# The last graph of a two-layer graph-attention kernel: its outputs written half by half in another order, reciprocals spread by ScalarE, and the range check in three parts

## The chip, the core and the metric

The kernel runs on one core of a Trainium2 chip. The core has five engines that run their own instruction streams side by side: TensorE (PE, matrix products; PEld is its loading of weights), VectorE (DVE), ScalarE (ACT), GpSimd (POOL) and SyncE (SP, which here only issues DMAs). They wait for one another through semaphores. SBUF is the on-chip memory with 128 partitions, PSUM the accumulators that TensorE writes. The metric is the device time of one execution in microseconds (us), of which the median of several runs is taken; a smaller number is better.

## What is computed

The input is 64 graphs of 256 nodes with 512 features each, and a 0/1 adjacency matrix for each graph; all is float32. Two attention layers follow one another.

```python
# layer 0
feat_proj = feats @ fc_w.T + fc_b
logits = (feat_proj @ q_w.T + q_b) + transpose(feat_proj @ k_w.T + k_b)
masked = leaky_relu(logits + (1 - adj) * -1e9, 0.01)
x = softmax(masked) @ feat_proj + feats
# layer 1, 8 heads of 64 features
Q, K, V = x @ W_q + b_q, x @ W_k + b_k, x @ W_v + b_v
scores = Q K^T / 8 + (x @ w_g[:D])_i + (x @ w_g[D:])_j + b_g + log(adj + 1e-9)
out = softmax(scores) @ V + x
```

## The kernel before, in words

Two graphs make a group, so there are 32 groups (`NG = 32`, `GP = 2`), and each group has four tiles of 128 nodes (`T = 4`). The loop over groups is unrolled. In step g the group g (called F) goes through layer 0 and the projections of layer 1, while group g-1 (A) goes through most of its attention, group g-2 (D) through what is left of it, and group g+1 (X) has its data loaded. The order of all instructions is written out by hand: strings such as `"pv.p2 scores:0 pv.p6"` name methods of a group, and every engine takes its instructions in exactly this order (`manual_schedule`). The projections are made from seven block products instead of eight (`pv.p1` to `pv.p7`, `Product.add`, line 412), with sums on DVE (`pv.sum_10` and so on, line 443) and copies from PSUM on ACT (line 429).

In the last step (g = 31) there is no group behind, so group 31 finishes its whole attention there. For each graph `gr` (0 or 1) and each half of the heads `hg` (0 or 1):

- `scores:u`, u = 2*gr + hg: PE makes the scores (line 859), ACT the exponentials (line 873);
- `factor:u:jc` multiplies them by the adjacency (DVE, line 879); `both:u` adds the two tiles (DVE, line 886);
- `sums_1:0` and `sums_of_e:1` add the weights over the columns by matmuls (lines 962 and 978), and ACT copies the sums to SBUF (`sms`, lines 969 and 985);
- `attend:gr` makes the weighted sums of values for both halves (PE, line 899), each copied from PSUM to the tile `oTs` by ACT (line 906);
- `ratios_t` transposes the sums in blocks of 32 (DVE, line 1023); `ratios_r` takes their reciprocal (line 996) and spreads it over `recip1` by one copy of all partitions and four of 32 partitions each, which overwrite parts of the first (lines 999 and 1002, all on DVE);
- `finish:gr` does for each half in turn: transposes the attended values (line 1033), multiplies by the reciprocals (line 1034) and adds the residual (line 1040), all on DVE with 512 columns each, and then stores the graph by four DMAs (line 1049), for graph 0 from SyncE's queue, for graph 1 from SyncE's and ScalarE's in turn.

Group 30 (A) finishes its second graph at the start of that stretch: `totals_1 ratios:1` (lines 927 and 942), `turn:1 divide:1 complete:1 store:1` (lines 991, 1011, 1019).

The softmaxes of the fast path take no maximum off. Instead, `in_range` compares every reciprocal with 1e-20 and 1e25 (`is_ge` at line 1058, `is_le` at line 1059), takes the minimum of the outcomes over the columns (line 1063) and the minimum with earlier outcomes (line 1065). `recip0` holds layer 0's reciprocals (4 columns for a group), `recip1` layer 1's (64 columns for a group, four groups at a time). The last call covers groups 30 and 31: 8 columns of layer 0 and 128 of layer 1. Then PE transposes the outcome (line 1096), DVE reduces it and writes an integer flag (lines 1100 and 1101), every engine loads the flag (line 1366) and branches on it (line 1368): a general version of the whole computation runs if any reciprocal was out of range, else the program ends.

The functions that the diff touches follow.

Of the kernel before, what the change touches and what calls it, by code (L numbers as in the profile page):

```python
# [10 lines left out]
F32 = mybir.dt.float32  # L11
I32 = mybir.dt.int32
AF = mybir.ActivationFunctionType
ALU = mybir.AluOpType
# [3 lines left out]
P = 128  # L18
# [7 lines left out]
def kernel(  # L26
# [64 lines left out]
    nc = tc.nc  # L91
    NB, N, D = x.shape
    NH = 8
    HD = D // NH
    B = 32
    RS = P // 4
    NC = D // P
    TPG = N // P
    GP = 2
    T = GP * TPG  # L100
    TOK = GP * N
    NG = NB // GP
# [10 lines left out]
    both = [i for i, a in enumerate(act_sets.SETS) if a.name == "natural_log_exp_and_others"]  # L113
    nc.scalar.add_instruction(
        mybir.InstLoadActFuncSet(
            name=nc.get_next_instruction_name(), act_func_set_id=both[0], ins=[], outs=[]
# [43 lines left out]
    NR = 4  # L160
    recip0 = const.tile([P, NG, T], F32, tag="recip0", name="recip0")
    recip1 = const.tile([P, NR, GP, NC, N // B], F32, tag="recip1", name="recip1")

    def fast():
        main = ExitStack()
        with main:
            one = main.enter_context(tc.tile_pool(name="one", bufs=1))
            wts = main.enter_context(tc.tile_pool(name="wts", bufs=1))
            two = main.enter_context(tc.tile_pool(name="two", bufs=2))
# [9 lines left out]
            def bank(name):  # L179
                return ps.tile([P, 512], F32, tag="bank", name=name)  # L180
# [64 lines left out]
            def columns(rows, cols, name):  # L245

                n = rows.shape[0]
                pt = bank(name)
                nc.tensor.transpose(pt[:, 0:n], rows, ident[0:n, 0:n])
                nc.vector.tensor_copy(cols, pt[:, 0:n])  # L250
# [138 lines left out]
            class Product:  # L389
# [5 lines left out]
                scores = False  # L395
# [133 lines left out]
            class Group:  # L529
# [357 lines left out]

                def attend(self, gr):

                    g = self.g  # L890
                    self.oTs[gr] = one.tile([P, 2, 512], F32, tag="oTs", name=f"oTs_{g}_{gr}")
                    for hg in range(2):
                        po = bank(f"oT_{g}_{gr}_{hg}")
                        oT = po.rearrange("p (r i) -> p r i", r=2)
                        for pr in range(2):
                            for jc in range(TPG):
                                for par in range(2):
                                    h = 4 * hg + 2 * pr + par
                                    nc.tensor.matmul(  # L899
                                        oT[par * HD : (par + 1) * HD, pr, :],  # L900
                                        lhsT=self.v[:, gr * TPG + jc, ts(h, HD)],
                                        rhs=self.e[2 * gr + hg, jc][:, par, pr, :],
                                        start=(jc == 0),
                                        stop=(jc == TPG - 1),
                                    )
                        nc.scalar.copy(self.oTs[gr][:, hg, :], po)  # L906

                def parts(self, u):

# [83 lines left out]
                def ratios_r(self, gr):  # L993
                    g, nb = self.g, N // B
                    rc = two.tile([P, 2, nb], F32, tag="rc", name=f"rc_{g}_{gr}")
                    nc.vector.reciprocal(rc, self.st.rearrange("p (b c) -> p c b", c=B)[:, 0:2, :])

                    rs = recip1[:, g % NR, gr].rearrange("p (h n) b -> p h n b", h=2)
                    nc.vector.tensor_copy(rs, rc.unsqueeze(2).to_broadcast([P, 2, 2, nb]))
                    for q in range(4):  # L1000
                        m = q ^ 1
                        nc.vector.tensor_copy(
                            rs[q * B : (q + 1) * B, :, m % 2, :], rc[m * B : (m + 1) * B]
                        )
                    self.rs = recip1[:, g % NR, gr]
# [16 lines left out]
                    self.st = one.tile([P, N], F32, tag="sms1", name=f"st_{self.g}_{gr}")  # L1022
                    nc.vector.transpose(self.st, self.sms1[gr])

                def finish(self, gr):


                    g, nb = self.g, N // B
                    self.osb[gr] = two.tile([P, NC * N], F32, tag="osb", name=f"osb_{g}_{gr}")
                    for hg in range(2):  # L1030
                        o = self.osb[gr][:, ts(hg, 512)]
                        blocks = o.rearrange("p (m c) -> p m c", c=B)
                        nc.vector.transpose(o, self.oTs[gr][:, hg, :])  # L1033
                        nc.vector.tensor_tensor(  # L1034
                            blocks, blocks,
                            self.rs[:, ts(hg, 2)].rearrange("p n b -> p (n b)").unsqueeze(2).to_broadcast(
                                [P, 2 * nb, B]
                            ), ALU.mult,
                        )
                        nc.vector.tensor_tensor(o, o, self.xb[gr][:, ts(hg, 512)], ALU.add)  # L1040
                    self.store(gr, 2 * (nc.sync, nc.scalar) if gr else 4 * (nc.sync,))

                def store(self, gr, queues=4 * (nc.sync,)):
                    dst = of[ts(self.g * GP + gr, N), :].rearrange(
# [3 lines left out]
                    for q in range(P // B):  # L1048
                        queues[q].dma_start(dst[q], src[q * B : (q + 1) * B])

            def in_range(lo, hi, name):

                n0, n1 = (hi - lo) * T, (hi - lo) * GP * NC * N // B
                ok = one.tile([P, n0 + n1], F32, tag="junk", name=f"ok_{name}")
                for src, a, b in ((recip0[:, lo:hi].rearrange("p g t -> p (g t)"), 0, n0),
                                  (recip1[:, lo % NR : lo % NR + hi - lo].rearrange(
                                      "p g a h b -> p (g a h b)"), n0, n0 + n1)):
                    nc.vector.tensor_scalar(ok[:, a:b], src, R_LOW, None, ALU.is_ge)
                    nc.vector.scalar_tensor_tensor(
                        ok[:, a:b], src, R_HIGH, ok[:, a:b], ALU.is_le, ALU.mult  # L1060
                    )
                okp = const.tile([P, 1], F32, tag=f"okp_{name}", name=f"okp_{name}")
                nc.vector.tensor_reduce(okp, ok, AX.X, ALU.min)
                if "all" in checked:
                    nc.vector.tensor_tensor(okp, okp, checked["all"], ALU.min)
                checked["all"] = okp

            def attention_and_layer_0(D, A, F, X):

# [21 lines left out]

            def check_ranges():

                in_range(NG - NR // 2, NG, "last")
                pk = bank("pok")
                nc.tensor.transpose(pk[0:1, 0:P], checked["all"], ident)

                def flag_ready():
                    oks = one.tile([1, 2], F32, tag="oks", name="oks")
                    nc.vector.tensor_reduce(oks[:, 0:1], pk[0:1, 0:P], AX.X, ALU.min)  # L1100
                    nc.vector.tensor_copy(flag, oks[:, 0:1])

                return flag_ready

            checked = {}

            def step(d, a, f, n, check):


# [13 lines left out]
                D, A, F, X = of(d), of(a), of(f), of(n)  # L1123
# [25 lines left out]
                X("dot_k:2 dot_k:3")  # L1149
                F("turn_residual:0")  # L1150
                if n is None:
                    A("attend:1 totals_1 ratios:1 turn:1 divide:1 complete:1 store:1")
                    F("residual:1 turn_residual:1")

                    F("pv.p2 scores:0 pv.p6 pv.sum_00 factor:0:0 factor:0:1 scores:1 both:0 pv.p7")
                    F("factor:1:0 factor:1:1 both:1 scores:2 pv.p5 sums_1:0 scores:3 pv.sum_11")
                    F("ratios_t:0 ratios_r:0 factor:2:0 factor:2:1 pv.p3 pv.p4 factor:3:0 pv.sum_10")
                    F("factor:3:1 attend:0 finish:0 sums_of_e:1 attend:1")
                    F("ratios_t:1 ratios_r:1 finish:1")
                    check_ranges()()  # L1160
                    return
                X("mask add_eps")
# [7 lines left out]
            with tc.manual_schedule(engines=ENGINES):  # L1170
                f = Group(0)
                f.x, f.a = x_0, adj_0

                warm = bank("warm")
                for n in range(6):
                    nc.tensor.matmul(warm[:, 0:P], lhsT=ident, rhs=ident, start=True, stop=True)
                columns(rows_0, cols_0, "cols_0")
                rows_qk = rows_of_x()
                k_constant = constant()
                d, a, a_w = None, None, {}  # L1180
                for g in range(NG):
                    n = Group(g + 1) if g + 1 < NG else None

                    def check():

                        if d is not None and (d.g % NR == NR - 1 or d.g == NG - NR // 2 - 1):
                            in_range(d.g // NR * NR, d.g + 1, f"{d.g}")

                    step(d, a, f, n, check)
                    d, a, f = a, f, n  # L1190
# [215 lines left out]
```

## Time and profile before

| | us |
|---|---|
| median of 3 runs | 2311.21 |
| lowest and highest of them | 2310.70, 2311.36 |
| the profiled execution's own time | 2310.62 |
| its span, first to last instruction | 2308.80 |
| PE busy in the span | 2294.2 (99%) |
| DVE busy | 2124.2 (92%) |
| ACT busy | 1071.8 (46%) |

The span was taken from one profiled execution by the hardware profiler, so single durations come from that execution. "Busy" is the time in which an engine ran an instruction; loads of registers, branches and semaphore waits aren't counted. The chain of waits follows the work that ended last back from the end: at each step to whatever released an instruction, or to the instruction before it on its engine. In a timeline line, the columns are the start in us, the time in us, the engine, the line of the code, the operation, its output and input tiles with their shapes, and how often it ran in a row; in brackets stands how long the engine was idle before it and what ended that. The engine names with a q (PEldq, DVEq) are the engines' instruction sequencers. The last TensorE product ahead of the final check ends at about 2297.1, the integer flag is written at 2302.82 to 2302.96, and the span ends at 2308.80.

### The profile page before, as it was taken

The page shows a single profiled execution, that of the slowest core. Times are in us where ns is not written, and L with a number is a line of the kernel's source. Part 1 is how long each engine was busy: PE and PEld are TensorE (multiplying, and loading weights), DVE is VectorE, ACT ScalarE, POOL GpSimd, SP SyncE. Part 2 cuts the span into 40 slices and gives each one's busy share as a digit, 9 for nine tenths or more (in the row PEclk, how much of TensorE's full clock was granted, in tenths as well). Part 3 has the DMA queues.
Part 4 walks back from the last instruction along what each step waited for, and adds up shares of the span by engine and source line. Part 5 has one row for each costly group of instructions (what it writes and reads, how often), then busy time and mean ns, then how long its engine had stood idle before and what let it go on. Part 6 is the DMA issues. An engine that isn't in the chain of part 4 may idle for free.

```text
span 2308.8 us, 33613 instructions
## 1 busy us (share of the span) xinstructions
PE 2294.2 (99%) x12618; PEld 1905.2 (83%) x12618; DVE 2124.2 (92%) x3180; ACT 1071.8 (46%) x1865; POOL 121.9 (5%) x120
## 2 busy tenths in 40 slices
PE   9999999999999999999999999999999999999997
PEld 6888888888888888888888888888888888888885
DVE  6899999999999999999999999999999999999997
ACT  3544444454445444454444454444544445444443
POOL 0000000000000000000000000000000000000000
PEclk9999999999999999999999999999999999999999
DMA  4122332223322233232233232332222323223312
GB/s 133 46 61 73 78 76 66 70 61 85 79 73 61 61 78 78 74 68 61 69 78 83 60 75 63 79 78 74 64 60 74 78 73 70 65 64 81 84 46 38
DMA packets 517264, 163.84 MB, mean 71 GB/s; under 512 B 415188, under 2 KB 478696, under 8 KB 517096
## 3 DMA queue, kind: packets, MB, share of 16 engines
q1 hardware_dynamic: 514440, 160.32, 28.8%
q8 instruction: 102, 1.67, 0.3%
q10 hardware_dynamic: 2656, 1.31, 0.2%
q14 instruction: 66, 0.54, 0.1%
HBM read 95.43 MB, written 66.12 MB: 70 GB/s over the span
## 4 chain that ended last, share of the span: by engine, by line
PE 98%; DVE 1%; DMA 0%; ACT 0%; issue 0%; ACTq 0%; DVEq 0%
PE pv L412 17%; PE pq L412 17%; PE pf L412 16%; PE pk L412 16%; PE sc L859 11%; PE oT L899 10%; PE y L689 9%; PE fp L718 1%; DMA fc_nat<-in_L_gnn_fc_w_dram 0%; PE rc L637 0%; DVE osb L1034 0%; PE tot L927 0%; DVE osb L1040 0%; PE xTp L705 0%; DVE osb L1033 0%; DVE x L756 0%
## 5 line engine op out<-in xcount | busy, mean ns | idle before, releaser
L873 ACT ACTIVATE e<-sc,c 128x1024 f32<-128x1024 f32 x254 | 269.0, 1110 | 79.2 <-PE sc L859 77.6
L879 DVE TENSOR_TENSOR e<-e,am 128x1024 f32<-128x1024 f32 x254 | 297.7, 1213 | 0.4 <-ACT e L873 0.4
L859 PE MATMUL sc<-qT,kT 64*128 64x256 f32 x2048 | 255.8, 390 | 0.3 <-ACT e L873 0.3
L899 PE MATMUL oT<-e,v 128*64 128x256 f32 x2032 | 233.4, 382 | 0.0
L859 PEld LDWEIGHTS sc<-qT,kT 64*128 64x128 f32 x2048 | 187.3, 187 | 52.6 <-issue 32.7
L495 POOL TENSOR_TENSOR pf_s<-pf_s,x 128x512 f32<-128x512 f32 x93 | 118.4, 1273 | 2106.1 <-ACT pf_s L494 2038.8
L689 PE MATMUL y<-e,x 128*128 128x256 f32 x992 | 225.6, 381 | 0.0
L899 PEld LDWEIGHTS oT<-e,v 128*64 128x64 f32 x2032 | 140.2, 137 | 85.3 <-issue 10.7
L689 PEld LDWEIGHTS y<-e,x 128*128 128x128 f32 x992 | 186.4, 190 | 23.7
L432 ACT ACTIVATE pq_s<-pq,cols 128x256 f32<-128x256 f32 x192 | 80.5, 470 | 249.1 <-PE pq L412 249.1
L494 ACT ACTIVATE pf_s<-pf,recip 128x256 f32<-128x256 f32 x186 | 77.9, 470 | 197.6 <-PE pf L412 197.6
L917 DVE TENSOR_REDUCE part<-est 128x32 f32<-128x1024 f32 x124 | 151.3, 1220 | 4.3
L916 DVE STREAM_TRANSPOSE est<-es 128x1024 f32<-128x1024 f32 x124 | 152.2, 1227 | 0.0
L886 DVE TENSOR_TENSOR es<-e,e 128x1024 f32<-128x1024 f32 x126 | 149.3, 1205 | 1.1
L695 ACT COPY yT<-y 128x512 f32<-128x512 f32 x124 | 72.6, 585 | 131.7 <-PE y L689 130.9
L429 ACT COPY pk_s<-pk 128x512 f32<-128x512 f32 x96 | 56.3, 586 | 165.7 <-PE pk L412 159.0
L906 ACT COPY oTs<-oT 128x512 f32<-128x512 f32 x128 | 75.0, 586 | 118.0 <-PE oT L899 97.3
L412 PE MATMUL pk<-t1b,wk 128*128 128x256 f32 x512 | 121.1, 380 | 0.4 <-DVE kT L443 0.4
L412 PE MATMUL pv<-wv,t1b_c 128*128 128x256 f32 x512 | 121.1, 380 | 0.0
L412 PE MATMUL pv<-wv,t1b 128*128 128x256 f32 x512 | 121.0, 380 | 0.0
L412 PE MATMUL pq<-x1T,wq 128*128 128x256 f32 x512 | 121.0, 379 | 0.0
L412 PE MATMUL pk<-x1T,wk 128*128 128x256 f32 x512 | 121.0, 379 | 0.0
(181 smaller groups left out, 4506.3 us busy)
## 6 DMA issues: line engine op xcount, KB each, us to landing
x<-in_x_dram SPq DMA_DIRECT2D x32, 1024.0 KB, 5.1
out_dram<-osb SPq DMA_DIRECT2D x254, 128.0 KB, 3.1
xd<-xt SPq DMA_DIRECT2D x124, 256.0 KB, 2.0
x1T<-xd SPq DMA_DIRECT2D x496, 64.0 KB, 1.9
adj<-in_adj_dram SPq DMA_DIRECT2D x128, 128.0 KB, 3.5
qrow<-q SPq DMA_DIRECT2D x31, 256.0 KB, 3.9
fc_nat<-in_L_gnn_fc_w_dram ACTq DMA_DIRECT2D x4, 256.0 KB, 3.8
wq<-in_L_gnn_W_q_dram SPq DMA_DIRECT2D x1, 1024.0 KB
```

The costliest lines, as they stand in the source:

```text
L412: nc.tensor.matmul(o, lhsT=lk[:, ts(m, P)] if len(lk.shape) == 2 else lk[:, m], rhs=rk, start=(start and m == 0 and k == 0), stop=(m == 1 ...
L432: nc.scalar.activation(dst[:, m], src[:, m], AF.Identity, bias=self.bias[:, 2 * o + m : 2 * o + m + 1],)
L494: nc.scalar.mul(s[:, m], src[:, m], self.recip[:, TPG * k + m : TPG * k + m + 1])
L495: nc.gpsimd.tensor_tensor(s, s, self.out(o, k), ALU.add)
L689: nc.tensor.matmul(y[:, ts(gr, N)], lhsT=self.x[:, gr * TPG + j, ts(c, P)], rhs=self.e0[:, j, gr, :], start=(gr == 0 and j == 0), stop=(gr ...
L859: nc.tensor.matmul(sc[:, par, pr, :], lhsT=self.kT[rows, 2 * hg + pr, ts(t, P)], rhs=self.qT[rows, 2 * hg + pr, ts(gr, N)], start=True, st ...
L873: nc.scalar.activation(e, sc, AF.Exp, bias=self.c[:, t : t + 1], scale=SCALE)
L879: nc.vector.tensor_tensor(ef, ef, self.am[:, jc, u // 2, :].unsqueeze(1).to_broadcast([P, 4, N]), ALU.mult,)
L886: nc.vector.tensor_tensor(self.esum[u], self.e[u, 0], self.e[u, 1], ALU.add)
L899: nc.tensor.matmul(oT[par * HD : (par + 1) * HD, pr, :], lhsT=self.v[:, gr * TPG + jc, ts(h, HD)], rhs=self.e[2 * gr + hg, jc][:, par, pr, :],
L916: nc.vector.transpose(turned, self.esum[u].rearrange("p a b i -> p (a b i)"))
L917: nc.vector.tensor_reduce(self.part[:, hg, :], turned.rearrange("p (m c) -> p m c", c=B), AX.X, ALU.add,)
```

## The change

Four things are edited, all of which act in the last step only.

- `attend` and `finish` are cut into units of one half: `attend_unit`, `turn_unit` (transpose into the output tile), `finish_unit` (multiply and add). The new order in the last step is: both halves of graph 0 attended, half 0 turned and finished, half 1 turned; then the sums of graph 1, their transpose and reciprocals; then half 1 of graph 0 finished and graph 0 stored; then for graph 1: half 0 attended and turned, half 1 attended, half 0 finished, half 1 turned and finished, stored.
- In `ratios_r` the five copies that spread the reciprocals are given to ScalarE instead of VectorE, for both graphs. The reciprocal itself stays on VectorE.
- `in_range` takes any list of sources. Its last call is cut in three: "late" (layer 0 of groups 30 and 31 and layer 1 of the first graph of group 30) ahead of group 30's `attend:1`, "later" (the second graph of group 30) behind `both:1`, and "last" (group 31, 64 columns) where the single call was.
- `finish_unit` reads `recip1` by its own index instead of the attribute `self.rs`.

The order of the units on PE stays as it was. The diff, cut to its core:

```diff
                 def attend(self, gr):
+                    for hg in range(2):
+                        self.attend_unit(gr, hg)
+
+                def attend_unit(self, gr, hg):
...
-                    nc.vector.tensor_copy(rs, rc.unsqueeze(2).to_broadcast([P, 2, 2, nb]))
+                    nc.scalar.copy(rs, rc.unsqueeze(2).to_broadcast([P, 2, 2, nb]))
                     for q in range(4):
                         m = q ^ 1
-                        nc.vector.tensor_copy(
+                        nc.scalar.copy(
                             rs[q * B : (q + 1) * B, :, m % 2, :], rc[m * B : (m + 1) * B]
                         )
...
-                def finish(self, gr):
...
+                def turn_unit(self, gr, hg):
+                    if hg == 0:
+                        self.osb[gr] = two.tile(
+                            [P, NC * N], F32, tag="osb", name=f"osb_{self.g}_{gr}"
+                        )
+                    nc.vector.transpose(self.osb[gr][:, ts(hg, 512)], self.oTs[gr][:, hg, :])
+
+                def finish_unit(self, gr, hg):
+                    nb = N // B
+                    o = self.osb[gr][:, ts(hg, 512)]
+                    blocks = o.rearrange("p (m c) -> p m c", c=B)
+                    rs = recip1[:, self.g % NR, gr]
+                    nc.vector.tensor_tensor(
+                        blocks, blocks,
+                        rs[:, ts(hg, 2)].rearrange("p n b -> p (n b)").unsqueeze(2).to_broadcast(
+                            [P, 2 * nb, B]
+                        ), ALU.mult,
+                    )
+                    nc.vector.tensor_tensor(o, o, self.xb[gr][:, ts(hg, 512)], ALU.add)
...
+                def store_by_both(self, gr):
+                    self.store(gr, 2 * (nc.sync, nc.scalar))
...
-            def in_range(lo, hi, name):
+            def in_range(name, *sources):
...
-                in_range(NG - NR // 2, NG, "last")
+                in_range("last", of_layer_1(NG - 1, NG))
...
                 if n is None:
+                    in_range("late", of_layer_0(NG - 2, NG), of_layer_1(NG - 2, NG - 1, slice(0, 1)))
                     A("attend:1 totals_1 ratios:1 turn:1 divide:1 complete:1 store:1")
                     F("residual:1 turn_residual:1")
 
                     F("pv.p2 scores:0 pv.p6 pv.sum_00 factor:0:0 factor:0:1 scores:1 both:0 pv.p7")
-                    F("factor:1:0 factor:1:1 both:1 scores:2 pv.p5 sums_1:0 scores:3 pv.sum_11")
+                    F("factor:1:0 factor:1:1 both:1")
+                    in_range("later", of_layer_1(NG - 2, NG - 1, slice(1, 2)))
+                    F("scores:2 pv.p5 sums_1:0 scores:3 pv.sum_11")
                     F("ratios_t:0 ratios_r:0 factor:2:0 factor:2:1 pv.p3 pv.p4 factor:3:0 pv.sum_10")
-                    F("factor:3:1 attend:0 finish:0 sums_of_e:1 attend:1")
-                    F("ratios_t:1 ratios_r:1 finish:1")
+                    F("factor:3:1 attend:0 turn_unit:0:0 finish_unit:0:0 turn_unit:0:1")
+                    F("sums_of_e:1 ratios_t:1 ratios_r:1 finish_unit:0:1 store:0")
+                    F("attend_unit:1:0 turn_unit:1:0 attend_unit:1:1 finish_unit:1:0")
+                    F("turn_unit:1:1 finish_unit:1:1 store_by_both:1")
                     check_ranges()()
                     return
```

More of the change, by code (lines that the diff above doesn't have):

```diff
@@ L888, in attend @@
                 def attend(self, gr):
+                    for hg in range(2):
+                        self.attend_unit(gr, hg)
+                def attend_unit(self, gr, hg):
                     g = self.g
[L891 to L906, printed above, removed]
+                    if hg == 0:
+                        self.oTs[gr] = one.tile([P, 2, 512], F32, tag="oTs", name=f"oTs_{g}_{gr}")
+                    po = bank(f"oT_{g}_{gr}_{hg}")
+                    oT = po.rearrange("p (r i) -> p r i", r=2)
+                    for pr in range(2):
+                        for jc in range(TPG):
+                            for par in range(2):
+                                h = 4 * hg + 2 * pr + par
+                                nc.tensor.matmul(
+                                    oT[par * HD : (par + 1) * HD, pr, :],
+                                    lhsT=self.v[:, gr * TPG + jc, ts(h, HD)],
+                                    rhs=self.e[2 * gr + hg, jc][:, par, pr, :],
+                                    start=(jc == 0),
+                                    stop=(jc == TPG - 1),
+                                )
+                    nc.scalar.copy(self.oTs[gr][:, hg, :], po)
                 def parts(self, u):
@@ L1023, in ratios_t @@
                     nc.vector.transpose(self.st, self.sms1[gr])
-                def finish(self, gr):
[L1028 to L1038, printed above, removed]
-                        )
-                        nc.vector.tensor_tensor(o, o, self.xb[gr][:, ts(hg, 512)], ALU.add)
-                    self.store(gr, 2 * (nc.sync, nc.scalar) if gr else 4 * (nc.sync,))
+                def turn_unit(self, gr, hg):
+                    if hg == 0:
+                        self.osb[gr] = two.tile(
+                            [P, NC * N], F32, tag="osb", name=f"osb_{self.g}_{gr}"
+                        )
+                    nc.vector.transpose(self.osb[gr][:, ts(hg, 512)], self.oTs[gr][:, hg, :])
[11 more added lines that the diff above has]
+                    nc.vector.tensor_tensor(o, o, self.xb[gr][:, ts(hg, 512)], ALU.add)
                 def store(self, gr, queues=4 * (nc.sync,)):
@@ L1049, in store @@
                         queues[q].dma_start(dst[q], src[q * B : (q + 1) * B])
-            def in_range(lo, hi, name):
[L1053 to L1057, printed above, removed]
+                def store_by_both(self, gr):
+                    self.store(gr, 2 * (nc.sync, nc.scalar))
+            def in_range(name, *sources):
+                ends = [0]
+                for src in sources:
+                    ends.append(ends[-1] + src.shape[1])
+                ok = one.tile([P, ends[-1]], F32, tag="junk", name=f"ok_{name}")
+                for src, a, b in zip(sources, ends, ends[1:]):
                     nc.vector.tensor_scalar(ok[:, a:b], src, R_LOW, None, ALU.is_ge)
@@ L1066, in in_range, with of_layer_0, of_layer_1 @@
                 checked["all"] = okp
+            def of_layer_0(lo, hi):
+                return recip0[:, lo:hi].rearrange("p g t -> p (g t)")
+            def of_layer_1(lo, hi, graphs=slice(0, GP)):
+                return recip1[:, lo % NR : lo % NR + hi - lo, graphs].rearrange(
+                    "p g a h b -> p (g a h b)"
+                )
             def attention_and_layer_0(D, A, F, X):
@@ L1186, in check @@
                         if d is not None and (d.g % NR == NR - 1 or d.g == NG - NR // 2 - 1):
-                            in_range(d.g // NR * NR, d.g + 1, f"{d.g}")
+                            lo, hi = d.g // NR * NR, d.g + 1
+                            in_range(f"{d.g}", of_layer_0(lo, hi), of_layer_1(lo, hi))
                     step(d, a, f, n, check)
```

## The prediction

> **What bounds the kernel now.** I read four views. First the page's busy line and its chain:
>
> ```profile
> PE 2294.2 (99%) x12618; PEld 1905.2 (83%) x12618; DVE 2124.2 (92%) x3180; ACT 1071.8 (46%) x1865; POOL 121.9 (5%) x120
> PE 98%; DVE 1%; DMA 0%; ACT 0%; issue 0%; ACTq 0%; DVEq 0%
> ```
>
> PE sets the end for 98% of the span. The diff leaves every step but the last one alone (`attend` is only cut in two, the check inside the loop keeps its instructions), so all that can move lies in the last 45 us. There the timeline of all engines shows who ends last (start, length in us, engine, line, operation):
>
> ```profile
> 2291.70 0.59 ACT L906 COPY oTs<-oT 128x512 f32<-128x512 f32 x1 [1.14 <-PE oT L899]
> 2292.67 0.70 DVE L1033 STREAM_TRANSPOSE osb<-oTs 128x512 f32<-128x512 f32 x1
> 2293.58 0.37 ACT L985 COPY sms<-sm 128x256 f32<-128x256 f32 x1 [1.30 <-PE sm L978]
> 2294.74 0.43 DVE L1023 STREAM_TRANSPOSE st<-sms 128x256 f32<-128x256 f32 x1
> 2295.21 0.25 DVE L996 RECIPROCAL rc<-st 128x16 f32<-128x16 f32 x1
> 2295.44 0.58 ACT L906 COPY oTs<-oT 128x512 f32<-128x512 f32 x1 [1.49 <-PE oT L899]
> 2295.50 0.18 DVE L999 COPY recip<-rc 128x32 f32<-128x32 f32 x1
> 2295.71 0.70 DVE L1002 COPY recip<-rc 32x16 f32<-32x16 f32 x4
> 2296.45 0.71 DVE L1033 STREAM_TRANSPOSE osb<-oTs 128x512 f32<-128x512 f32 x1
> ...
> 2301.14 0.29 DVE L1059 SCALAR_TENSOR_TENSOR ok_last<-recip,ok_last 128x128 f32<-128x128 f32 x1
> 2301.46 0.29 DVE L1063 TENSOR_REDUCE okp_last<-ok_last 128x1 f32<-128x136 f32 x1
> 2301.79 0.16 DVE L1065 TENSOR_TENSOR okp_last<-okp_last,okp 128x1 f32<-128x1 f32 x1
> 2302.07 0.08 PEld L1096 LDWEIGHTS pok<-ident,okp_last 128*1 128x1 f32 x1 [5.41 <-issue]
> ```
>
> From 2290.59 to 2301.95 DVE works without a real pause. It is the bound of the last 12 us; PE and ACT wait. PE's last matmuls before the check end at about 2297.1. Third, the view of the line with the final branch on the flag says what follows the flag, which is written until 2302.96:
>
> ```profile
> L1368 DVEq COMPARE_BRANCH x1: 72/72/72, 2304.0 to 2304.0; - x1
> L1368 PEldq COMPARE_BRANCH x1: 3697/3697/3697, 2304.0 to 2304.0; - x1
> ```
>
> Each engine reads the flag in 0.91 to 0.95 us and branches; PE's branch takes until 2307.7, the others' 0.05 to 0.07 us, and an all-engine barrier of 1.1 us ends the span at 2308.8. The stores land by about 2305.7 (SyncE's waits for them end there), 2 us before PE's branch does. So the **flag** sets the end, 5.84 us ahead of it, not the output.
>
> **The change, part by part.** Times are of the profiled execution (span 2308.80, time 2310.62).
>
> *Check part "late"* (8 + 32 columns, six DVE instructions) goes behind the residual's transpose that ends at 2266.17. Rows of the present check: 0.17 and 0.17 us for 8 columns, 0.22 and 0.29 for 128 (so some 0.18 and 0.19 for 32), reduction at most 0.29, minimum 0.16; with 0.02 between them 1.1 to 1.2 us. DVE's own timeline has room at both new places:
>
> ```profile
> 2268.03 0.36 DVE L942 RECIPROCAL recip<-tot 128x32 f32<-128x32 f32 x1 [1.86 <-PE tot L927]
> ...
> 2282.12 0.69 DVE L443 TENSOR_TENSOR v<-pv,pv_s 128x512 f32<-128x512 f32 x1 [0.82 <-ACT pv_s L429]
> ```
>
> An idle time of 1.86 us covers "late": 0. Without that cover it would cost its 1.2 us, since PE's column sums at 2281.39 wait for DVE's sum of the weights with almost nothing to spare. *"later"* (32 columns, four instructions: 0.18 + 0.19 + 0.20 + 0.16 and gaps, 0.8 us) goes into the 0.82 us ahead of `pv.sum_11`. An overrun has 0.1 us before the sums' transpose at 2282.94 feels it, and after that the next part frees 0.9 us: 0.
>
> *Reciprocals of graph 0*: five copies leave DVE (2283.70 to 2284.62) and go to ACT behind the two exponentials that end at 2285.70. DVE's factors start 0.94 us earlier, but `pv.sum_10` needs PE's product p4, which ends at 2288.04, and the first turn needs ACT's copy after PE's attend at 2289.97. PE runs without a pause there, so the 0.9 us become a wait on PE: 0. On ACT about 1 us is queued ahead of the copy `v<-pv` (2286.36), now done by about 2287.1; its reader is PE at 2293.44 and PE may want that bank at 2287.97: hidden.
>
> *The last graph's order.* Up to the turn of half 0:1 (ends 2293.37) nothing moves. Then DVE goes straight to the transpose of the sums, which has to wait for ACT's copy (2293.58 + 0.37 = 2293.95): an **added idle of 0.6 us**, with multiply and add of half 0:1 and store 0 queued behind it. From 2293.98: transpose 0.45, reciprocal 0.25 (until 2294.71), multiply and add of half 0:1 (0.69 + 0.69 and gaps) until 2296.15. DVE would be free 0.30 before the 2296.45 of now.
>
> But ACT has five copies to do from 2294.75, and the copy of half 1:0 behind them (ready at 2295.42, now at 2295.44). The trace has no such small copy from SBUF on ACT. Nearest: `tot<-rc` (L647), 32x4 from PSUM, 152 ns, four in 0.64 us, a step of 0.16; and SBUF against PSUM on ACT at 128x512, L378 622 ns against L429 586, 0.04 more. Below, 5 x 0.15 = 0.75; above, five of the 265 ns of ACT's 128x128 row (L663) and 0.04 each, 1.5. I take 5 x 0.20 = 1.0, next to L647: ACT is free at 2295.75, the copy of half 1:0 runs until 2296.33 (little overlap counted), the turn starts at 2296.35. **Gain 0.10**; the ends are 0.30 (DVE bound) and a loss of 0.4.
>
> [...]
>
> From the turn of 1:0 six DVE instructions follow in 4.23 us as now (2296.45 to 2300.68); the half 1:1 is copied by 2297.74, in time. Store 0 is issued at 2296.15 instead of 2294.85: its four issues (2.77 us) leave SP by 2298.9, and its packets by about 2300.4, ahead of store 1 (issued from 2300.6, packets from 2301.7): 0.
>
> *The last check* has 64 columns instead of 8 + 128: six instructions from 2300.60 to 2301.95 become four. Interpolated: 0.19 + 0.23 + 0.22 + 0.16 and gaps, ending 0.81 after the add instead of 1.27: **gain 0.46**. The transposed minimum, the reduction and the flag follow unchanged.
>
> Sum: 0.10 + 0.46 = **0.56 us** earlier flag, and end. On the profiled execution 2310.62 - 0.56 = 2310.06. That execution was 0.59 below the runs' median of 2311.21 (2310.70 to 2311.36); from the median I predict **2310.65 us**, 0.02% less. A measurement of this kernel can tell about 0.2% (4.6 us) from no change, so this is "same".
>
> **Rivals.**
>
> A, *the branch's fetch meets the stores*. In the DMA row of the last stretch, packets of the stores run until about 2304.8, then 0.2 us nothing, then the instruction queues' packets from 2305.0. A flag 0.56 earlier asks for them at 2304.5, into the stores, which move by the turn's 0.10 alone. If they must wait for the stores' end, the gain is 0.10 + 0.2 = 0.3: 2310.9. For it: the queues follow one another closely. Against: 1.0 us between branch and packets is also what store 1 needs from issue to packets (2300.7 to 2301.7), so it may be mere delay.
>
> [...]
>
> B, *the wait on ACT takes the copies' place* and the kernel is slower than before. Place: ACT between the reciprocal and the copy of half 1:0. Price: every 0.1 us of the five copies over 1.0 moves the turn, the flag and the end by 0.1. It decides from 1.56 us for the five (0.31 each), where it eats the 0.46 of the check as well. The upper end plus waits between copies that overwrite part of the first one's area, 0.4 each or 2.0 us, gives +0.44: 2311.65. For it: four of the five write over the first one's result. Against: L647's step of 0.16.
>
> C, *tiles move*. Two more one-column tiles in the constants can shift what is allotted behind them by bytes. If that changed a matmul by 0.4 ns (x 12618 = 5 us), it would pass 4.6 us either way: 2316 or 2306. Against: matmuls of one shape on different tiles agree, 379 to 381 ns. It decides only from a change of 0.1% of a matmul.
>
> D, *no effect*: DVE waits for ACT's copies before half 0:1 as well (same tile `recip1`, other columns). Then multiply starts at 2295.8, the turn at 2297.1, 0.67 later, less 0.46: 2311.4. Against: the turn of half 0:0 ran at 2290.59, before half 0:1 of the same tile `oTs` was written, so parts are told apart.
>
> **How the numbers follow.** Forecast (gain 0.4 to 0.76) 0.55; A 0.15; B 0.15; D 0.10; C 0.05. All but C lie within 0.2%; C is split, 0.03 slower, 0.02 faster: faster 0.02, same 0.95, slower 0.03. Range: lowest time seen 2310.62 less the largest gain 0.76, and highest 2311.36 plus B's 0.44, each widened by 0.4 for the spread of four runs (0.74): 2309.5 to 2312.2.
>
> **What would show it.** In the profile after: a DVE wait of 0.6 us for `sms`; five ACT copies of about 0.2 us starting near 2294.8; the turn of 1:0 near 2296.35; four check instructions of 0.8 us; flag near 2302.4; PE's branch still 3.7 us; DVE's idle 1.86 and 0.82 us filled. Copies over 0.3 us, or a late `oTs` copy, speak for B; a longer branch for A; other matmul durations for C; a multiply after 2295.7 for D. A time outside by more than 1 us with the tail as written would make the whole picture wrong.

## The result, and the profile after

The changed kernel took 2314.56 us (median of 21 runs, 2313.36 to 2315.81); the kernel before, measured alongside, took 2311.56 (21 runs, 2309.90 to 2313.38). The ratio is 1.0014 [1.0008, 1.0020]: 3.0 us slower, where 0.56 us less had been predicted. It lies within the 0.2% that the prediction called "same", but outside its range of 2309.5 to 2312.2. The profiled execution of the changed kernel took 2313.46 us (span 2311.7) against 2310.62 (2308.8).

The page of the changed kernel, its busy line and its chain:

```profile
PE 2292.5 (99%) x12618; PEld 1900.5 (82%) x12618; DVE 2123.0 (92%) x3178; ACT 1074.4 (46%) x1875; POOL 122.0 (5%) x120
PE 98%; DVE 1%; DMA 0%; ACT 0%; issue 0%; ACTq 0%
```

PE still fills the span and matmuls take what they took (the five largest groups of L412 in both pages 379 to 380 ns), so nothing here tells where 3 us came from. Note only two small numbers: DVE has two instructions fewer (3178 against 3180), ACT ten more.

The two executions start differently (the first loads), and behind them stand at a nearly constant distance: the first exponential comes 0.98 us earlier in the changed kernel, long before any edited step, and the last one begins at 2284.59 us before and at 2283.54 after, 1.05 earlier. That distance isn't the change's. So all readings below count from that exponential. Three points cut the tail: last exponential, end of the flag's write, end of the span.

| us | exponential to flag | flag to end | sum |
|---|---|---|---|
| before | 18.37 | 5.88 | 24.26 |
| after | 17.95 | 10.19 | 28.14 |

**Up to the flag the kernel is faster by 0.42; behind it, it is slower by 4.31.** Here is the stretch up to the flag, in the timeline of all engines of the changed kernel:

```profile
2292.93 0.45 DVE L1027 STREAM_TRANSPOSE st<-sms 128x256 f32<-128x256 f32 x1 [0.61 <-ACT sms L989]
2293.41 0.25 DVE L1000 RECIPROCAL rc<-st 128x16 f32<-128x16 f32 x1
...
2293.70 0.22 ACT L1003 COPY recip<-rc 128x32 f32<-128x32 f32 x1 [0.80 <-DVE rc L1000]
2293.95 0.84 ACT L1006 COPY recip<-rc 32x16 f32<-32x16 f32 x4
...
2294.82 0.59 ACT L910 COPY oTs<-oT 128x512 f32<-128x512 f32 x1
...
2295.44 0.71 DVE L1034 STREAM_TRANSPOSE osb<-oTs 128x512 f32<-128x512 f32 x1 [0.50 <-ACT oTs L910]
...
2299.59 0.19 DVE L1068 TENSOR_SCALAR ok_last<-recip 128x64 f32<-128x64 f32 x1
...
2301.35 0.14 DVE L1119 CAST flag<-oks 1x1 int32<-1x1 f32 x1
```

The reader sees the added wait for `sms` (0.61), the five copies on ACT (1.09 us from first start to last end), ACT's copy of half 1:0 right behind them, DVE idle for 0.50 until it is there, and a last check that is shorter. Behind the flag the view of the line with the branch, and that of the barrier at the end, read (duration in ns least/median/most, then the first and last start):

```profile
L1392 PEldq COMPARE_BRANCH  x1: 4621/4621/4621, 2302.6 to 2302.6; - x1
...
L1392 DVEq EVENT_SEMAPHORE  x1: 21/21/21, 2307.7 to 2307.7; - x1
```

```profile
L1425 DVEq DRAIN  x2: 10/72/135, 2310.8 to 2311.2; - x2
```

PE's branch takes 4.62 us instead of 3.70. Then comes the larger piece: VectorE runs one semaphore instruction at 2307.7, and its very next instruction, a drain, only at 2310.8. The drain takes 135 ns, where 10 to 17 are usual. In the kernel before the drain starts 0.11 us after the semaphore instruction (before rounding):

```profile
L1368 DVEq EVENT_SEMAPHORE  x1: 21/21/21, 2307.8 to 2307.8; - x1
```

```profile
L1401 DVEq DRAIN  x2: 10/14/17, 2308.0 to 2308.4; - x2
```

Nothing in the program makes VectorE wait between them.

### The profile page after: what moved, and what is told of

Same layout as the page of the kernel before. It is cut to its first block, busy times and chain, and to the rows that moved or that the text cites. A ratio compares the mean times of both kernels' runs of the same rounds, so it can differ in the third digit from the quotient of the medians.

```text
span 2311.7 us, 33619 instructions
## 1 busy us (share of the span) xinstructions
PE 2292.5 (99%) x12618; PEld 1900.5 (82%) x12618; DVE 2123.0 (92%) x3178; ACT 1074.4 (46%) x1875; POOL 122.0 (5%) x120
## 4 chain that ended last, share of the span: by engine, by line
PE 98%; DVE 1%; DMA 0%; ACT 0%; issue 0%; ACTq 0%
PE pv L412 17%; PE pq L412 17%; PE pf L412 16%; PE pk L412 16%; PE sc L859 11%; PE oT L903 10%; PE y L689 9%; PE fp L718 1%; DMA fc_nat<-in_L_gnn_fc_w_dram 0%; PE rc L637 0%; PE tot L931 0%; DVE x L756 0%; DVE part L921 0%; DVE est L920 0%; PE xTp L705 0%; PE row L273 0%
## 5 line engine op out<-in xcount | busy, mean ns | idle before, releaser
L412 PE MATMUL pk<-t1b,wk 128*128 128x256 f32 x512 | 121.1, 379 | 0.4 <-DVE kT L443 0.4
L412 PE MATMUL pv<-wv,t1b_c 128*128 128x256 f32 x512 | 121.1, 379 | 0.0
L412 PE MATMUL pv<-wv,t1b 128*128 128x256 f32 x512 | 121.1, 379 | 0.0
L412 PE MATMUL pq<-x1T,wq 128*128 128x256 f32 x512 | 121.0, 379 | 0.0
L412 PE MATMUL pk<-x1T,wk 128*128 128x256 f32 x512 | 121.0, 379 | 0.0
```

What stands on the lines that cost most here:

```text
L412: nc.tensor.matmul(o, lhsT=lk[:, ts(m, P)] if len(lk.shape) == 2 else lk[:, m], rhs=rk, start=(start and m == 0 and k == 0), stop=(m == 1 ...
```

## Experiments

The theory that came out of this comparison has two parts. *One:* the taken branch jumps past the general version, so an engine whose next instructions aren't loaded has them fetched by DMA (in the kernel before, PE's branch took 3.70 us, and the first instruction packet started 1.04 us after it), VectorE in blocks that come as packets of 8 KB (the page of the kernel before has 66 of them on queue 14 for the 7922 instructions that the trace lists on the four engines besides PE, so some 120 in each, as an estimate; six of them start at 69.64, 196.91, 320.18, 443.49, 568.91 and 693.36 us, when ScalarE has begun 64, 192, 321, 448, 576 and 703 instructions, 127 to 129 apart). VectorE's stream has two instructions fewer, and so the tail behind the branch happens to be cut: its semaphore instruction is the last of one block, its drain the first of the next, and that block is asked for only once VectorE has begun on the first. In the changed kernel VectorE's semaphore instruction stands 6.21 us behind the flag, instruction packets follow at 6.81 and 6.86, and the drain comes at 9.32. *Two:* the rest of the loss comes from the output stores, beside which the first fetch has to get through. Rivals: ScalarE's ten added instructions did the first; the later store 0 did the second; or the new order simply cost what was measured.

**Two idle DVE instructions added to the changed kernel** among the initial loads bring VectorE's stream back to its old length.

```diff
+for n in range(2):
+    nc.vector.tensor_copy(eps, eps)
 columns(rows_0, cols_0, "cols_0")
```

> The changed kernel with two idle VectorE copies of one column at the start, so that VectorE's instruction stream is as long as before the change. Theory T (the time after the flag is instruction fetch: VectorE's last instructions fall on two fetched blocks of 128 instructions): the pause of 3.1 us between VectorE's semaphore instruction behind the branch and its drain goes, flag to end falls from 10.2 to about 7.0 us, time about 2311.4, which is 3 us less than the changed kernel. Rival R1 (the stores of the last graphs drain later, nothing else): flag to end stays near 10 us, time about 2314.5.

Measured: 2312.17 against 2311.24 us, ratio 1.0002 [0.9993, 1.0011]; exponential to flag 17.96, flag to end 7.23, which is 2.96 less than in the changed kernel. Two instructions more give back 2.1 us of the medians' distance (3.00 to 0.93); the kernel with idle ACT instructions instead, measured at the same time (below), is 2.8 us slower than this one. The view of the end barrier:

```profile
L1427 DVEq DRAIN  x2: 10/14/17, 2309.2 to 2309.6; - x2
```

The 135 ns are gone, and so is the gap: the drain follows the semaphore instruction (2309.1) directly. What stays is 7.23 - 5.88 = 1.35 us.

**Two DVE instructions taken from the kernel before**, out of an earlier range check; nothing of the change is in it.

```diff
+if name == "29" and a == 0:
+    continue
 nc.vector.tensor_scalar(ok[:, a:b], src, R_LOW, None, ALU.is_ge)
...
-nc.vector.tensor_reduce(okp, ok, AX.X, ALU.min)
+nc.vector.tensor_reduce(okp, ok[:, n0:] if name == "29" else ok, AX.X, ALU.min)
```

> The kernel before, with the check of groups 28 and 29 leaving out layer 0's reciprocals: two VectorE instructions fewer near 2249 us, where they delayed nothing, so VectorE's stream has the length of the changed kernel's. Theory T: flag to end grows from 5.9 to about 9 us and the time by 3 us to about 2314.5, with the order of the last graph untouched. Rival R1: flag to end stays 5.9 us, time 2311.3.

Measured: 2313.96 against 2311.24 us, ratio 1.0013 [1.0004, 1.0022]; 18.38 to the flag, then 8.39, which is 2.51 more than before. Less work, and the loss is there without any part of the change. The two views, of the branch and of the barrier:

```profile
L1370 DVEq EVENT_SEMAPHORE  x1: 21/21/21, 2308.4 to 2308.4; - x1
```

```profile
L1403 DVEq DRAIN  x2: 10/72/134, 2311.0 to 2311.4; - x2
```

The same gap (2.6 us) and the same long drain. That two instructions' place in VectorE's stream costs this much is settled by these two runs, in both directions; that the time is a fetch is read from the instruction packets and from the run with the short general version below.

**Three idle ACT instructions added to the changed kernel** shift ScalarE's stream, whose tail was cut by a block edge there too.

```diff
+for n in range(3):
+    nc.scalar.copy(minus, minus)
 columns(rows_0, cols_0, "cols_0")
```

> The changed kernel with three idle ScalarE copies of one column at the start: ScalarE's last instructions move away from the block's end, VectorE's stay. Theory T: ScalarE's drain comes within 0.2 us of its semaphore instruction instead of 4.3 us after it, but the end stays with VectorE: flag to end 10 us, time about 2314.5. Rival R2 (ScalarE's fetch delays VectorE's): flag to end falls by 1 us or more.

Measured: 2314.99 against 2311.24 us, ratio 1.0016 [1.0007, 1.0025]; flag to end 10.11 against 10.19. In the changed kernel ScalarE's drain was late as well (5.94 us behind the flag, 135 ns), but it fetched while PE's branch was still under way. The padding didn't spare it the wait: now its semaphore instruction, too, lies behind the edge (5.93 us behind the flag instead of 1.62). VectorE's drain, at 9.24 us, decides all the same.

**No stores of the last graph**, and four idle DVE instructions to keep VectorE off the edge, in the changed kernel. It leaves that graph out of the output.

```diff
-F("turn_unit:1:1 finish_unit:1:1 store_by_both:1")
+F("turn_unit:1:1 finish_unit:1:1")
...
+for n in range(4):
+    nc.vector.tensor_copy(eps, eps)
```

> The changed kernel with four idle VectorE copies at the start (VectorE off the block's end) and without the four stores of the last graph, which is left out of the output. Theory A (the fetch of the branch's target waits for the stores' packets): the first instruction packets come about 1.0 us after the branch or sooner instead of 2.1, PE's branch takes 3.5 us instead of 4.6, flag to end about 5.5 us, time about 2310. Rival (the fetch has a delay of its own): first packets 2.1 us after the branch, PE's branch 4.6 us, flag to end 7 us, time 2311.4.

Measured: 2311.22 against 2311.24 us, ratio 0.9999 [0.9990, 1.0009]; 17.96 to the flag and 5.39 behind it. PE's branch took 3717 ns, the loads of the flag 463 to 543 ns (905 to 946 in the kernel before, 989 to 1078 in the changed one). So all of the remaining 1.35 us, and 0.5 more, hang on the stores of the last graph (this is read in the tail; the medians of this run and of the padded kernel lie 0.95 us apart, which their intervals don't resolve). What about them had changed? The DMA view of both kernels, in a window of 12 us with the end of the flag's write in its middle (40 slices of 0.3 us; the busy share in tenths, then GB/s). Before:

```profile
DMA  9999998000000000199999999913200000000040
GB/s 191 173 188 184 159 198 148 1 0 0 0 0 0 0 0 0 32 201 186 198 171 154 211 213 205 161 17 82 55 0 0 0 0 0 0 0 0 0 109 0
```

After:

```profile
DMA  0049999869999960006999887999995400000000
GB/s 0 0 65 144 143 141 144 131 81 167 170 167 146 143 104 2 0 0 95 148 143 142 130 128 102 170 173 154 145 139 96 120 0 0 0 0 0 0 0 0
```

The same bytes flow at some 140 GB/s instead of some 185, in both stores. Before, the last store packet ends 1.93 us behind the flag, and the instruction packets (the slices with 82 and 55) come at 2.10, 1.04 us after PE's branch. After, the last one ends at 3.47, and the instruction packets come at 3.28, 2.12 us after the branch. The stores are slower, although they issue the same DMAs. What did move are the tiles: `okp_late` and `okp_later` are two new tiles in the constants, 32 bytes each, and `osb`, the source of the stores, went from byte 188160 of each partition to 188224.

**The changed kernel with all tiles at their old addresses**: the two new tiles take over the places of older ones that are dead, with the two DVE instructions as above.

```diff
+tag = {"late": "okp_3", "later": "okp_7"}.get(name, f"okp_{name}")
-okp = const.tile([P, 1], F32, tag=f"okp_{name}", name=f"okp_{name}")
+okp = const.tile([P, 1], F32, tag=tag, name=f"okp_{name}")
```

> The changed kernel with VectorE's stream as long as before (two idle copies at the start), and with the two added one-column tiles of the range check put where two dead ones lie, so that every tile has the address of the kernel before (the output tiles start at a multiple of 128 bytes again instead of 64 beyond one). Theory S (the stores' 128-byte packets are slower when they leave SBUF 64 bytes off, and the instruction fetch waits for them): packets of the last stores end about 1.0 us earlier, at some 2.4 us after the flag instead of 3.5; the branch's instruction packets come 1.0 to 1.3 us after the branch instead of 2.1; flag to end 6.0 to 6.3 us instead of 7.2; time about 2311.0, some 0.3 below the kernel before. Rival (the later store of graph 0 slows the stores, not the address): packets, branch and end stay as with the padding alone, 7.2 us from flag to end, 2312.1.

Measured: 2311.40 against 2311.19 us, ratio 1.0001 [0.9992, 1.0010]; 17.95 to the flag, 6.10 behind it. The last store packet ends 2.39 us behind the flag, the mean packet of the stores takes 11.8 to 12.6 ns as before, not 13.2 to 13.7, and the first instruction packet comes 1.26 us after the branch. The order of the stores here is that of the changed kernel, so a later store 0 isn't the cause. PE's branch, in the view of its line:

```profile
L1395 PEldq COMPARE_BRANCH  x1: 4037/4037/4037, 2305.1 to 2305.1; - x1
```

**The kernel before with one added tile of 64 bytes** in the constants, which nothing uses.

```diff
 def check_ranges():
+    const.tile([P, 16], F32, tag="shift", name="shift")
```

> The kernel before with 64 bytes more in the constants, nothing else: all tiles behind them move by 64 bytes. Theory S: packets of the output stores take 13.2 instead of 11.8 to 12.6 ns, the last one ends 1 us later after the flag (2.9 instead of 1.9 us), flag to end grows from 5.9 to about 6.9 us, time about 2312.2. Rival (the order of the stores): nothing moves, 2311.2.

Measured: 2311.95 against 2311.19 us, ratio 1.0004 [0.9995, 1.0013], which can't tell it from no change; but in the tail, flag to end is 6.72 instead of 5.88, with the last store packet's end at 2.96 us behind the flag and the first instruction packet 1.63 us after the branch. The line of the branch, and the page's line of the stores (KB of one, median us to landing), here and in the kernel before:

```profile
L1369 PEldq COMPARE_BRANCH  x1: 4297/4297/4297, 2304.6 to 2304.6; - x1
```

```profile
out_dram<-osb SPq DMA_DIRECT2D x254, 128.0 KB, 3.4
```

```profile
out_dram<-osb SPq DMA_DIRECT2D x254, 128.0 KB, 3.1
```

A tile without a reader costs the median store 0.3 us, which is hidden everywhere but at the end, where the tail grows by 0.83. Part two is thereby shown in both directions, for 1.13 of the 1.35 us.

From its first to its last packet, the store of graph 0 ran at 176 GB/s before and at 137 after, that of graph 1 at 180 and 131: ratios of 1.28 and 1.37. With the old addresses they are at 175 and 180 again. The time of a single packet rose by a tenth only. These runs show that 64 bytes do this; why, no run shows, and no offset but 64 bytes was tried.

**The five copies back on VectorE**, for both graphs, all else as in the changed kernel (the ten instructions also move VectorE's stream off the edge).

```diff
-nc.scalar.copy(rs, rc.unsqueeze(2).to_broadcast([P, 2, 2, nb]))
+nc.vector.tensor_copy(rs, rc.unsqueeze(2).to_broadcast([P, 2, 2, nb]))
...
```

> The changed kernel with the five copies that spread the reciprocals back on VectorE, its new order and its three checks kept. VectorE then has 0.9 us more ahead of the turn of half 1:0, and ScalarE copies half 1:0 without a queue in front: the turn starts 0.5 to 0.6 us later than in the changed kernel, and last exponential to flag is 18.45 to 18.55 us instead of 17.95. So the order alone would gain nothing over the kernel before (18.37), and the move to ScalarE is worth some 0.5. Rival (ScalarE's copies cost as much as they save): 17.95. Both instruction streams end away from a block's end here, so flag to end is 7.2 us and the time about 2312.6.

Measured: 2312.67 against 2311.19 us, ratio 1.0003 [0.9994, 1.0012]; 18.38 to the flag, 7.32 behind it. That is the same 18.37 as before: without the move to ACT, the new order spends all that the shorter check saves (the wait for `sms` is there, 0.61, and the copies are still on VectorE's path). The expectation had set it 0.1 higher. The move to ACT is worth the 0.42.

**The general version cut to one load and one store**, on top of the kernel with old addresses.

```diff
 def general(pool):
+    t = pool.tile([P, D], F32, tag="t", name="t")
+    nc.sync.dma_start(t, xf[0:P, :])
+    nc.sync.dma_start(of[0:P, :], t)
+    return
```

> The kernel of the run align_pad with the general fallback cut to a load and a store of one tile; the fallback isn't taken with these inputs, but is left incomplete. Theory F (the time after the flag is the fetch of the branch's target, because the fallback's code lies between): the target is then 2 instructions away, PE's branch takes 0.1 us instead of 3.7 to 4.6, and the end comes when the stores have landed, 3.5 to 4.2 us after the flag; time about 2309. Rival (a taken branch costs its 3.7 us whatever its distance): flag to end as with align_pad, 6 to 6.3 us.

Measured: 2309.15 against 2311.19 us, ratio 0.9993 [0.9984, 1.0002]; 17.85 to the flag, 4.26 behind it. The branch:

```profile
L1399 PEldq COMPARE_BRANCH  x1: 229/229/229, 2302.8 to 2302.8; - x1
```

The same instruction takes 0.23 us where its target is near and 3.4 to 4.9 us in the runs where the general version lies between. So the 3.7 us are the fetch, as the prediction supposed, and the end is then set by SyncE's wait for the stores (its drain comes 3.31 us behind the flag) and, a little, by a late last drain of ScalarE (135 ns). Behind such a branch, the crossing of a block edge cost 2.5 us (the kernel before with two instructions fewer) to 3.0 us (the changed kernel against the padded one).

**Both paddings, and the old addresses:** the kernel with old addresses and the three ACT instructions.

```diff
+for n in range(3):
+    nc.scalar.copy(minus, minus)
 columns(rows_0, cols_0, "cols_0")
```

> The changed kernel with every side effect undone: tiles at the addresses of the kernel before, two idle VectorE copies and three idle ScalarE copies at the start so that neither stream ends on a block's end. Theory (only VectorE's stream and the stores mattered): as align_pad, last exponential to flag 17.95 us, flag to end 6.0 to 6.1 us, so 24.0 us in all against 24.26 before, time 0.2 us below the kernel before. Rival (ScalarE's second block, whose drain came 0.02 us before VectorE's semaphore in align_pad, shares the fetch with VectorE's): flag to end 5.6 us or less, time 0.6 us below.

Measured: 2311.58 against 2311.06 us, ratio 1.0002 [0.9993, 1.0011]; 17.96 and 6.30, 0.2 more than without the ACT padding, so neither expectation came true. The ACT padding is no help: ScalarE's own target now lies outside what it has loaded (its semaphore instruction comes 4.91 us behind the flag, not 1.37), and with VectorE's fetch beside it, nothing gets earlier.

**The flag ahead of the stores.** The last check is cut in two and put where VectorE waits anyway, and the flag is written before the last half is finished, so that the fetch comes before the stores. Old addresses, four idle ACT instructions.

```diff
+in_range("last0", of_layer_1(NG - 1, NG, slice(0, 1)))
 F("sums_of_e:1 ratios_t:1 ratios_r:1 finish_unit:0:1 store:0")
+F("attend_unit:1:0")
+in_range("last", of_layer_1(NG - 1, NG, slice(1, 2)))
+F("turn_unit:1:0 attend_unit:1:1")
+flag_ready = check_ranges()
+F("finish_unit:1:0")
+flag_ready()
+F("turn_unit:1:1 finish_unit:1:1 store_by_both:1")
```

> The kernel align_both, with the last check cut in two (one for each graph of group 31, in VectorE's two pauses) and the flag written ahead of the last multiply and add, so that the branch doesn't wait for it: PE branches while VectorE still works, VectorE loads the flag right after the last add. Theory A strict (instruction packets of VectorE's branch wait until the last stores' packets have left, as in the changed kernel): the fetch begins near the stores' end, 4.0 us after the last add, and the end comes 7.6 us after it; VectorE's last add comes 0.9 us later, so the whole from last exponential to end is 24.3 to 24.7 us, time 0.1 to 0.5 us over align_both. Rival (the fetch goes between the stores' packets, 1.0 to 1.3 us after the branch): fetch 2.1 us after the last add, end 5.7 us after it, whole 22.8 us, time about 2310.

Measured: 2311.72 against 2311.06 us, ratio 1.0003 [0.9994, 1.0013]; the flag stands 14.71 us behind the exponential, the end 24.53 (24.26 in the kernel before). The fetches of PE and VectorE now come 1.04 and 1.05 us after their branches, ahead of the store packets. But ScalarE branches last, behind its store issues, and its fetch falls into the stores:

```profile
L1399 ACTq COMPARE_BRANCH  x1: 54/54/54, 2306.8 to 2306.8; - x1
...
L1399 ACTq EVENT_SEMAPHORE  x1: 17/17/17, 2310.7 to 2310.7; - x1
```

Between the two lie 3.9 us, hardly more than such a fetch took without stores beside it (3.8 us from VectorE's branch to its semaphore instruction in the kernel before). And this wait isn't what sets the end. SyncE ends last, with its waits for the stores and the semaphore instructions behind them:

```profile
L1399 SPq EVENT_SEMAPHORE  x8: 17/17/17, 2308.7 to 2310.3; - x8
```

Its last drain ahead of the barrier stands 9.09 us behind the flag, ScalarE's at 8.89. The sum lies where theory A had put it, but by luck: VectorE's fetch came ahead of the store packets, and the landing of the stores set the end.

**The same with ScalarE's target in reach**: no ACT padding, graph 0's five copies back on VectorE.

```diff
+copy = nc.scalar.copy if gr else nc.vector.tensor_copy
-nc.scalar.copy(rs, rc.unsqueeze(2).to_broadcast([P, 2, 2, nb]))
+copy(rs, rc.unsqueeze(2).to_broadcast([P, 2, 2, nb]))
...
```

> The kernel early_flag without the idle ScalarE copies and with graph 0's five small copies back on VectorE (0.9 us there, beside PE's product p4), so that ScalarE's stream ends inside a block that is already loaded, as in the kernel before. Theory (in early_flag ScalarE's late branch and its fetch set the end): ScalarE's semaphore instruction comes 0.4 us after its branch instead of 3.9, the end is then set by the landing of the stores, about 1.5 us after their last packet, and last exponential to end falls from 24.5 to 23.3 to 23.7 us; time 0.6 to 1.0 us below the kernel before. Rival (SyncE's late branch or the stores set the end anyway): 24.3 us or more, time as with early_flag, 2311.7.

Measured: 2311.70 against 2312.63 us (11 and 15 runs), ratio 0.9999 [0.9990, 1.0008]; the flag at 14.71, the end at 24.70. The sum was expected 1 us and more lower; this missed. The view of the branch's line:

```profile
L1398 SPq EVENT_SEMAPHORE  x8: 17/17/17, 2308.8 to 2309.3; - x8
...
L1398 ACTq EVENT_SEMAPHORE  x1: 17/17/17, 2306.1 to 2306.1; - x1
```

ScalarE's wait is gone (its semaphore instruction comes 0.5 us after its branch at 2305.6), and the end is no earlier: the rival was right. SyncE's waits for the stores end only at 2309.3, 23.2 us behind the exponential, as in the run before, and the barrier follows them in both. (The 0.17 us more in the end are ScalarE's last drain, 136 ns long and 0.3 us late, which looks like a block edge again.) The last add ends at 2302.93, 16.78 behind the exponential (16.09 in the kernel before), and the last store packet ends 5.5 us later (4.2 there). The trace shows where that time lies: 4049 of the 4096 packets of graph 1's store have started by 6.36 us behind the flag, the other 47 start only from 6.86 to 7.52, and three instruction packets that start between 6.07 and 6.39 take 0.65 to 0.85 us each. So these store packets seem to have stood behind a fetch; no run varied it. No version here is faster than the kernel before by more than its interval.

## Why the prediction was wrong, point by point

The step that failed is the last of the sum: "**0.56 us** earlier flag, and end". It carried the 5.84 us of "So the **flag** sets the end, 5.84 us ahead of it" over to the changed kernel as a constant, and gave the new lengths of the streams and the new places of the tiles no price there. The tail became 10.19 us (5.88 before, from times not rounded). The sum that the runs give: -0.42 up to the flag, +2.96 for VectorE's second block (undone by two idle instructions), +1.35 for the fetch behind slower stores (1.13 of it gone with the old addresses, 7.23 to 6.10), which is +3.89 in all in the profiled executions; medians differ by 3.0 [1.8 to 4.6 from the ratio's interval].

- *Last check, gain 0.46.* Right: from the turn of half 1:0 to the flag 6.51 became 6.05.
- *Turn of half 1:0, gain 0.10.* Wrong by size: a loss of 0.04 (11.86 to 11.90 us behind the exponential). The five copies took 1.09 us instead of 1.0: the rows here are 0.22 and four of 0.21.
- *"late" and "later" at no cost.* Right. In VectorE's timeline the idle time of 1.86 ahead of the reciprocal shrank, and the 0.82 ahead of the sum is filled:

```profile
2266.98 0.36 DVE L946 RECIPROCAL recip<-tot 128x32 f32<-128x32 f32 x1 [0.86 <-PE tot L931]
...
2281.07 0.69 DVE L443 TENSOR_TENSOR v<-pv,pv_s 128x512 f32<-128x512 f32 x1
```

- *Graph 0's reciprocals, 0.* Right: `pv.sum_10` now waits 1.07 us for PE.
- *Store 0 later, 0.* Right by itself: with the old addresses the same order of stores ran at full speed.
- *PE's branch "still 3.7 us".* Wrong: 4.62.
- *Rival A*, the fetch meets the stores. Right in kind, and with the old addresses in size too: the flag is earlier, the stores' end is not, and the tail grows by 0.22 (5.88 to 6.10) where A had 0.26. In the changed kernel the stores also ended 1.5 us later against the flag, and it was 1.35; A had them end when they did. The 1.0 us from branch to packets is mere delay, as was argued against A (1.04 before, 1.04 and 1.05 with the early flag), but in the changed kernel a wait comes on top: 2.12, with the fetch 0.2 us ahead of the stores' end. In the run with the early flag and no ACT padding it was rather store packets that came late, so which of the two goes first isn't settled here.
- *Rival B*, ACT's copies eat the gain: no; 0.21 each, far from 0.31. *Rival D*: no; the multiply of half 0:1 didn't wait for the copies.
- *Rival C*, tiles move. Right that they do (64 bytes), but looked for at the wrong reader: matmuls kept their 379 to 381 ns, while the stores' DMA, which reads the same tiles, slowed down.
- No rival had the block edge, which is the largest term. The profile held it in its 5.84 us: the page's count of instruction packets, and a branch on PE that took 3.7 us, pointed to fetches. The prediction counted instructions as work on an engine, not as places in a stream.

## What to carry to other kernels

Where a kernel ends behind a taken branch, price the instructions as a stream: two more or fewer on one engine can put its last instructions into a second fetched block, which cost 2.5 to 3.0 us here, six to seven times what the edit gained up to the flag. Before believing that a small loss comes from an edit, pad the streams by some idle instructions and pin the tiles to their old addresses, and time again. A new tile can move all tiles behind it (two of 32 bytes were enough here), so keep the sources of stores in short pieces where they were (here at byte 188160 for the last graph; 64 bytes further its stores ran at 131 instead of 180 GB/s), or reuse a dead tile's place.

## What the runs showed of the hardware that was not expected

- The first packet of instructions came 1.04 us after PE's branch in the kernel before, 0.17 us behind the last store packet, and 1.04 us after it with the early flag, ahead of the store packets; with later or slower stores it came 1.26 (old addresses), 1.63 (64 bytes added to the kernel before) and 2.12 us (changed kernel) after it. A second block of VectorE cost another 2.5 to 3.0 us, and its first instruction, a drain, took 135 ns instead of 10 to 17.
- A branch of PE took 0.23 us with a near target and 3.4 to 4.9 us with a far one.
- The last graph's stores, of 128-byte pieces, ran at 180 GB/s from byte 188160 of the partitions and at 131 from 188224.
- The load of the flag took 0.46 to 0.54 us without the last graph's stores, 0.91 to 0.95 in the kernel before, and 0.99 to 1.08 beside the slower stores of the changed kernel.
